# Two chained convolution layers on one core: the last three channel groups taken image by image, early loads in parts, outputs in blocks of 1024 columns

## The chip, the core and the metric

The kernel runs on one core of a Trainium2 chip. The metric is the device time of one execution in microseconds. Its engines are TensorE (PE in the profile; PEld is its weight load), VectorE (DVE), ScalarE (ACT), GpSimd (POOL) and SyncE (SP); 16 DMA engines move data between HBM and the on-chip memory (SBUF). SyncE, GpSimd and ScalarE can issue DMAs, each in the order of its own instructions.

## The reference

Input x is 4 images of 64 channels, 256 x 256, float32. Layer 0 is a long convolution: two small sine networks give, for every channel, a filter along the rows and one along the columns, and their outer product is convolved with the image through an FFT of double size; a bias times x is added. Layer 1 whitens the 64 channels: a covariance of every ninth pixel, its inverse square root by five Newton-Schulz steps, and a 64 x 64 product with every pixel.

```python
k = jnp.einsum('ijk,imk->ijmk', hx, hy)[0]
y = jnp.fft.irfft2(u_f * k_f, s=(fft_size, fft_size))[..., :L, :L]
out = y + x * bias[:, None, None]
...
x1 = jnp.transpose(x, (1, 0, 2, 3)).reshape(B, -1)
x1_s = x1[:, ::STRIDE ** 2]
mean1 = jnp.mean(x1_s, axis=-1, keepdims=True)
xc = x1 - mean1
cov = x1_s @ x1_s.T / x1_s.shape[1] + EPS * jnp.eye(B, dtype=x.dtype)
deconv = _isqrt_newton_schulz(cov, N_ITER)
out = deconv @ xc
```

## The kernel before, in words

**Layer 0.** The separable convolution is done as two products with Toeplitz matrices for each channel of each image. The work is cut in 32 steps (lines 107 and 108), a step being one group of 8 channels (index g, 0 to 7) of one image (n, 0 to 3). Groups 0 to 5 go group by group, all four images inside; groups 6 and 7 go image by image. Each step has four items of two channels (c = 0, 2, 4, 6). `group` (line 394) makes TensorE do the first product of one item together with the second product of the item two places before, so that an item is finished two groups after it was begun. A place is written (step, c), as in the table `early`. ScalarE copies the first products (line 409), VectorE adds x times the bias to the second ones, in place of x (line 412).

**Around it.** After each group SyncE's queue gets, in this order: two stores of the finished item to a DRAM scratch `y_d` (line 425, 1 KB a row), a load of two channels of x for the step two ahead, into one of four tiles (line 588), perhaps an eighth of a later group's Toeplitz matrices (line 594, by the table `blocks`, line 371) and perhaps an early load of the second layer (line 596, by the table `early`, line 378). The matrices lie in three tiles. VectorE also picks the pixels for the covariance by masked copies (line 319), which `pack` (line 385) hands out by a budget of 2.92 for each group. The covariance of an image (line 333, on TensorE) is placed one step behind the image's last group (line 571).

**Between the layers.** After the last item, TensorE picks the last pixels by products (line 300), makes the last covariance and goes through the Newton-Schulz chain (`whitening`, line 460), which gives W and a shift.

**Layer 1.** The 32 pieces (line 344) are 128 x 4096 numbers of `y_d` each, 2 MB: the two image halves by 64 channels as rows. For blocks of columns, four products with W fill two banks (line 635), ScalarE and VectorE add the shift and write them back in place (lines 639, 640), and the piece is stored to the output (line 645). The on-chip tiles of layer 0 that are done with serve as the homes of the pieces (line 347): 13 at a time, from the pools of the matrices (t), the samples (s), x (i) and one more (e). Nine of the first 13 are loaded by `early` before layer 0 ends, the others on line 614. Piece 13 and on is loaded (line 647) when the piece 13 before it has been stored. The outputs of piece 0 and of the last 13 are issued by SyncE, the others by GpSimd. A piece is 2 x 2048 columns: block w takes 512 of each half. Outputs go out in 4 DMAs for piece 0, 2 for piece 1 and for the last two, 1 for the others.

Of the kernel before, what the change touches and what calls it, by code (L numbers as in the profile page):

```python
# [38 lines left out]
F32 = mybir.dt.float32  # L39
I32 = mybir.dt.int32  # L40
AF = mybir.ActivationFunctionType
ALU = mybir.AluOpType
# [3 lines left out]
NB, C, L = 4, 64, 256  # L46
P, H2 = 128, 2
EMB, ORDER = 33, 64
PIX = L * L
CG = 8  # L50
# [4 lines left out]
EPS = 0.01  # L55
N_ITER = 5
GW = P + L
FP = 4096

TURN = 6.283185  # L60
# [4 lines left out]
def conv_whiten_kernel(ctx: ExitStack, tc: tile.TileContext, a: dict, out: bass.AP):  # L65
    nc = tc.nc
    x = a["x"]

    const = ctx.enter_context(tc.tile_pool(name="const", bufs=1))
    xpool = ctx.enter_context(tc.tile_pool(name="xpool", bufs=4))  # L70
    epool = ctx.enter_context(tc.tile_pool(name="epool", bufs=2))
    spool = ctx.enter_context(tc.tile_pool(name="spool", bufs=NB))
    tpool = ctx.enter_context(tc.tile_pool(name="tpool", bufs=3))
    o1pool = ctx.enter_context(tc.tile_pool(name="o1pool", bufs=4))
# [13 lines left out]
    cols = const.tile([P, 4], F32, tag="cols", name="cols")  # L88
# [9 lines left out]
    bias = const.tile([P, C], F32, tag="bias", name="bias")  # L98

    def load_x(t, g, n, c):  # L100
        nc.sync.dma_start(
            out=t[:, c : c + 2],
            in_=x[n, g][:, c : c + 2],
        )


    steps = [(g, n) for g in range(C // CG - 2) for n in range(NB)]
    steps += [(g, n) for n in range(NB) for g in range(C // CG - 2, C // CG)]

    x_tiles = [xpool.tile([P, CG, H2, L], F32, tag="in", name=f"x{u}") for u in range(4)]  # L110
    for c in range(0, CG, 2):
        load_x(x_tiles[0], *steps[0], c)
# [8 lines left out]
    for n in range(NB):  # L121
        t = spool.tile([P, FP], F32, tag="samp", name=f"samp{n}")
        samp.append(
# [31 lines left out]
    for i in range(3):  # L155
        for u in range(2):
# [3 lines left out]
            arg, k, nxt = (scratch[:, 2 + 3 * i + v, half] for v in range(3))  # L160
# [166 lines left out]
    def covariance(n):  # L327
# [15 lines left out]

    pieces = [(n, q) for n in range(NB) for q in range(PIX // H2 // FP)]


    homes = [
        {"t": (tpool, "toep"), "s": (spool, "samp"), "i": (xpool, "in"), "e": (epool, "extra")}[k]
        for k in "eetssiistitis"
    ]  # L350

    def load_y(i):
# [4 lines left out]
        nc.sync.dma_start(out=t, in_=y_d[n][:, q * FP : (q + 1) * FP])  # L357
        return t

    def load_next():  # L360
        loaded[len(loaded)] = load_y(len(loaded))

    loaded = {}
    todo = []
# [16 lines left out]
    orders = [list(range(L // HP)), list(reversed(range(L // HP)))]  # L381

# [174 lines left out]
    with tc.manual_schedule(  # L557
        engines={engines.PE, engines.SP, engines.DVE, engines.Activation, engines.Pool}
    ):
        toep = {0: new_toeplitz(0)}  # L560

        for f, lo, hi in ((0, 0, 2), (0, 2, 4), (0, 4, 6), (1, 0, 2), (0, 6, 8), (1, 2, 4), (1, 4, 8)):
            for half in range(2):
                load_toeplitz(toep[0], 0, f, half, lo, hi, nc.scalar if half else nc.sync)
        for c in range(0, CG, 2):
            load_x(x_tiles[1], *steps[1], c)
        for i, (g, n) in enumerate(steps):
            xt = x_tiles[i % 4]
            for c in range(0, CG, 2):
                item = (g, n, c, xt, [])  # L570
                if g == C // CG - 1 and n > 0 and c == 2:
                    covariance(n - 1)
                if len(pending) == 2:
                    group(item, pending.pop(0))
                else:
                    half_group(item, 0)
                pending.append(item)
                if i == 0 and c == 6:

                    fold = const.tile([P, C], F32, tag="fold", name="fold")  # L580
# [8 lines left out]
                if (i, c) in blocks:  # L589
                    tg, part = blocks[i, c]  # L590
# [24 lines left out]
        W, shift = whitening(i15, ones)  # L615


    halves = [slice(u * C, (u + 1) * C) for u in range(2)]
    for i, (n, q) in enumerate(pieces):
        yt = loaded.pop(i)  # L620

        v = yt.rearrange("p (v f) -> p v f", v=2)
        o = out[n, q].rearrange("p (v f) -> p v f", v=2)

        part = 512 if i == 0 else 1024 if i == 1 or i > len(pieces) - 3 else 2048
        for w in range(FP // 1024):


            cols = slice(w * 512, (w + 1) * 512)
            po = [  # L630
                psA.tile([P, 512], F32, tag="psA", name=f"po_{n}_{q}_{w}_{u}") for u in range(2)
            ]
            for k in range(2):
                for u in range(2):
                    nc.tensor.matmul(  # L635
                        po[u][halves[k]], lhsT=W[halves[u]], rhs=v[halves[u], k, cols],
                        start=True, stop=True,
                    )
            nc.scalar.activation(v[:, 0, cols], po[0], AF.Identity, bias=shift)  # L639
            nc.vector.tensor_scalar(v[:, 1, cols], po[1], shift, None, ALU.add)  # L640
            end = (w + 1) * 512
            if end % part == 0:

                issue = nc.sync if i == 0 or i + len(homes) >= len(pieces) else nc.gpsimd
                issue.dma_start(out=o[:, :, end - part : end], in_=v[:, :, end - part : end])  # L645
        if i + len(homes) < len(pieces):
            loaded[i + len(homes)] = load_y(i + len(homes))

# [57 lines left out]
```

## Time and profile before

| what | value |
|---|---|
| median of 3 runs | 902.66 us (902.32 to 902.82) |
| span of the profiled execution | 902.1 us |
| TensorE matmul busy | 781.2 us (87%) |
| VectorE busy | 581.5 us (64%) |
| ScalarE busy | 395.5 us (44%) |
| bytes moved by DMA | 285.61 MB, mean 317 GB/s |
| x loads (line 101) | 128 of 512 KB, median 5.3 us from issue to landing |
| `y_d` stores (line 425) | 256 of 256 KB, median 3.5 us |
| piece loads (line 357) | 32 of 2 MB, median 15.6 us |

The profile is one execution. It gives for each engine the busy time, in 40 equal slices of the span too; a chain of what released what, followed back from the end; groups of instructions by line with the idle time before them; and DMA traffic by queue and by issue. A busy share of one engine over the whole span says little here, since the two layers load the engines differently; the slices show that. "Share" of the DMA engines is the mean busy share of the 16. The profile's own execution is not among the three timed runs; its span counts from the first to the last instruction.

### The profile page before, as it was taken

The numbers are of one execution on the slowest core, as the hardware profiler recorded it, in microseconds if no ns is written. First come the engines' busy times: TensorE is split into PE (matmuls) and PEld (weight loads), VectorE is DVE, ScalarE is ACT, GpSimd is POOL, SyncE is SP. The second block draws the span as 40 slices with busy tenths as digits, with TensorE's granted clock in tenths as the row PEclk, the third lists the DMA queues.
The fourth block names the chain that finished last, engine by engine and source line by source line (L and its number), as shares of the span: only waits on it lengthen the run. The fifth ranks groups of instructions, "written<-read, shape, count | busy, mean of one in ns | idle before, by whom it ended". The sixth has DMA issues, their size and how long they took to land.

```text
span 902.1 us, 28046 instructions
## 1 busy us (share of the span) xinstructions
PE 781.2 (87%) x11928; PEld 647.5 (72%) x11928; DVE 581.5 (64%) x801; ACT 395.5 (44%) x676; POOL 14.5 (2%) x40
## 2 busy tenths in 40 slices
PE   8999999999999999999999999999999565666200
PEld 7999999999999999999999999999533111212000
DVE  3487778877888778877888877877688332233200
ACT  2655554545455555545454444442487232233200
POOL 1000000000000000000000000000010000000000
PEclk9999999999999999999999999999999766866755
DMA  7988889798788888888997899979999999999998
GB/s 209 327 262 252 242 261 271 234 273 251 247 263 261 244 264 259 258 250 267 293 275 241 285 351 356 335 237 390 375 401 429 430 432 432 429 434 430 430 430 355
DMA packets 117912, 285.61 MB, mean 317 GB/s; under 512 B 8891, under 2 KB 91116, under 8 KB 110108
## 3 DMA queue, kind: packets, MB, share of 16 engines
q1 hardware_dynamic: 113436, 244.94, 79.0%
q0 software_dynamic: 3056, 37.95, 10.0%
q8 instruction: 95, 1.56, 0.7%
q10 hardware_dynamic: 1296, 0.93, 0.4%
q14 instruction: 29, 0.24, 0.1%
HBM read 149.35 MB, written 134.44 MB: 315 GB/s over the span
## 4 chain that ended last, share of the span: by engine, by line
PE 74%; DMA 11%; another core or an unknown queue 7%; DVE 0%; issue 0%; SPq 0%; ACT 0%; POOLq 0%; DVEq 0%
PE p L220 64%; DMA out_dram<-yi 5%; DMA yi<-y_d 5%; PE po L635 4%; PE pc L333 2%; PE ph L252 1%; PE pk L300 1%; PE spin L442 1%; DMA toep<-g_d 0%; PE busy L152 0%; PE pm L158 0%; SPq L357 0%; DMA scratch<-in_zw_dram 0%; DVE yi L640 0%
## 5 line engine op out<-in xcount | busy, mean ns | idle before, releaser
L220 PE MATMUL p<-toep,x 64*64 64x64 f32 (+3 forms) x5040 | 579.5, 284 | 0.8 <-issue 0.8
L220 PE MATMUL p<-toep,o 64*64 64x64 f32 (+3 forms) x5040 | 579.5, 284 | 0.0
L220 PEld LDWEIGHTS p<-toep,x 64*128 64x128 f32 (+1 forms) x5040 | 535.7, 166 | 24.4 <-issue 1.3
L220 PEld LDWEIGHTS p<-toep,o 64*128 64x128 f32 (+1 forms) x5040 | 536.7, 166 | 10.7 <-issue 0.2
L409 ACT COPY o<-p 64x512 f32<-64x512 f32 x504 | 292.8, 581 | 294.2 <-PE p L220 286.6
L319 DVE COPY_PREDICATED samp<-mask,x 128x464 f32<-128x464 int32 (+3 forms) x351 | 297.2, 847 | 9.8 <-DVE x L412 0.2
L412 DVE SCALAR_TENSOR_TENSOR x<-x,bias,p 128x512 f32<-128x512 f32 x252 | 179.8, 744 | 121.3 <-PE p L220 117.3
L635 PE MATMUL po<-yi,chain 64*64 64x512 f32 x1024 | 143.7, 720 | 60.4 <-DMA yi<-y_d 60.4
L640 DVE TENSOR_SCALAR yi<-po,shift 128x512 f32<-128x512 f32 x128 | 96.1, 751 | 109.0 <-PE po L635 100.7
L635 PEld LDWEIGHTS po<-yi,chain 64*64 64x64 f32 x1024 | 48.0, 162 | 155.2 <-issue 150.5
L639 ACT ACTIVATE yi<-po,shift 128x512 f32<-128x512 f32 x128 | 88.0, 687 | 116.7 <-PE po L635 116.0
L333 PE MATMUL pc<-samp 128*64 128x65 f32 x464 | 14.9, 223 | 0.0
L333 PEld LDWEIGHTS pc<-samp 128*64 128x64 f32 x464 | 14.3, 137 | 0.3
L645 POOL DMA_DIRECT2D out_dram<-yi x19 | 10.5, 554 | 130.5 <-DMA out_dram<-yi 55.1
L606 POOL TENSOR_SCALAR chain<-ident 64x64 f32<-64x64 f32 x2 | 1.0, 519 | 606.6 <-PE ph L252 606.6
L286 DVE COPY o<-ph 64x256 f32<-64x256 f32 x8 | 3.4, 422 | 9.7 <-PE ph L252 9.6
L152 PE MATMUL busy<-idle 128*128 128x128 f32 x64 | 9.4, 307 | 0.0
L152 PEld LDWEIGHTS busy<-idle 128*128 128x128 f32 x64 | 8.9, 222 | 0.2 <-issue 0.2
L300 PE MATMUL pk<-x,pick 128*128 128x56 f32 (+1 forms) x72 | 8.3, 292 | 0.0
L300 PEld LDWEIGHTS pk<-x,pick 128*128 128x128 f32 x72 | 8.1, 192 | 0.1
L442 PE MATMUL spin<-ident 128*128 128x128 f32 x50 | 7.9, 292 | 0.0
L286 ACT COPY o<-ph 64x256 f32<-64x256 f32 x8 | 2.9, 368 | 10.7 <-DMA toep<-g_d 9.2
(93 smaller groups left out, 77.4 us busy)
## 6 DMA issues: line engine op xcount, KB each, us to landing
x<-in_x_dram SPq DMA_DIRECT2D x128, 512.0 KB, 5.3
y_d<-x SPq DMA_DIRECT2D x256, 256.0 KB, 3.5
yi<-y_d SPq DMA_DIRECT2D x32, 2048.0 KB, 15.6
out_dram<-yi POOLq DMA_DIRECT2D x17, 2048.0 KB, 67.7
out_dram<-yi SPq DMA_DIRECT2D x11, 2048.0 KB, 32.9
toep<-g_d SPq DMA_DIRECT2D x28, 256.0 KB, 6.3
toep<-g_d SPq DMA_DIRECT2D x29, 192.0 KB, 5.7
out_dram<-yi SPq DMA_DIRECT2D x4, 1024.0 KB, 32.8
```

Of the source, the lines that this page charges most:

```text
L152: nc.tensor.matmul(p, lhsT=idle[:, 0:P], rhs=idle[:, P : 2 * P], start=True, stop=True)
L220: mm = nc.tensor.matmul(ps[q : q + w, m, HP * k : L], lhsT=src[parts, k // 2, m * P + q : m * P + q + w], rhs=t[parts, : stop : -1] if k e ...
L300: nc.tensor.matmul(pk[:, b, :, 0:nj], lhsT=pick[:, (s - b) % STEP, :], rhs=yt[:, cs, b, s : s + STEP * (nj - 1) + 1 : STEP], start=(s == 0 ...
L319: nc.vector.copy_predicated(dst, m, src)
L333: nc.tensor.matmul(pc[half], lhsT=samp[n][:, b, j, 0:C], rhs=samp[n][:, b, j, :], start=(b == 0 and j < 2), stop=(b == H2 - 1 and j >= NJ ...
L409: nc.scalar.copy(o1[to], units[u][0][0][fr])
L412: nc.vector.scalar_tensor_tensor(x2[:, c2 + u], x2[:, c2 + u], bias[:, ch : ch + 1], units[u][1][0], ALU.mult, ALU.add,)
L442: nc.tensor.matmul(p, lhsT=ident, rhs=ident, start=True, stop=True)
L635: nc.tensor.matmul(po[u][halves[k]], lhsT=W[halves[u]], rhs=v[halves[u], k, cols], start=True, stop=True,)
L639: nc.scalar.activation(v[:, 0, cols], po[0], AF.Identity, bias=shift)
L640: nc.vector.tensor_scalar(v[:, 1, cols], po[1], shift, None, ALU.add)
L645: issue.dma_start(out=o[:, :, end - part : end], in_=v[:, :, end - part : end])
```

## The change

- Groups 5, 6 and 7 go image by image, not 6 and 7 alone: image 0 is complete after 23 steps instead of 26. The covariance of an image stays one step behind its last group.
- x has three tiles instead of four, and is loaded one step ahead instead of two; x of the last step is loaded in the first half of step 30. The pool `e` has three tiles instead of two.
- The tables change: Toeplitz blocks of groups 4 to 7 are loaded earlier (and two at a time in places for group 7), in another order of their eight parts; ten pieces are loaded early, the first at (23,4), instead of nine from (26,4). Those before step 30 are loaded in four DMAs of 1024 columns each.
- A piece is cut in four blocks of 1024 adjacent columns, a block being 2 x 512. A slice of the output is then contiguous in each row. The number of output DMAs of each piece stays.

```diff
+LATE = 3
-    xpool = ctx.enter_context(tc.tile_pool(name="xpool", bufs=4))
-    epool = ctx.enter_context(tc.tile_pool(name="epool", bufs=2))
+    xpool = ctx.enter_context(tc.tile_pool(name="xpool", bufs=3))
+    epool = ctx.enter_context(tc.tile_pool(name="epool", bufs=3))
...
-    steps = [(g, n) for g in range(C // CG - 2) for n in range(NB)]
-    steps += [(g, n) for n in range(NB) for g in range(C // CG - 2, C // CG)]
+    steps = [(g, n) for g in range(C // CG - LATE) for n in range(NB)]
+    steps += [(g, n) for n in range(NB) for g in range(C // CG - LATE, C // CG)]
...
+    def x_of(i):
+        return x_tiles[(i + 1) % 3]
...
-        for k in "eetssiistitis"
+        for k in "eeessstititis"
...
-        nc.sync.dma_start(out=t, in_=y_d[n][:, q * FP : (q + 1) * FP])
+        width = FP // parts
+        for at in range(0, FP, width):
+            nc.sync.dma_start(
+                out=t[:, at : at + width], in_=y_d[n][:, q * FP + at : q * FP + at + width]
+            )
...
-    for g in range(1, C // CG):
-        first = 16 * g - 14 if g < C // CG - 1 else 16 * g - 22
-        for part in range(8):
-            k = first + (part * 12 // 8 if g < C // CG - 2 else part)
-            blocks[k // 4, k % 4 * 2] = (g, part)
+    for g, (first, groups) in {
+        1: (2, 12), 2: (18, 12), 3: (34, 12), 4: (46, 12), 5: (57, 12), 6: (69, 12), 7: (82, 5)
+    }.items():
+        for at, part in enumerate((0, 2, 1, 3, 4, 6, 5, 7)):
+            k = first + at * groups // 8
+            blocks.setdefault((k // 4, k % 4 * 2), []).append((g, part))
...
-        (26, 4): 1, (27, 0): 1, (27, 4): 1, (28, 0): 1, (29, 2): 1, (30, 0): 1, (31, 0): 1, (31, 2): 1, (31, 4): 1
+        (23, 4): 1, (24, 0): 1, (24, 4): 1, (25, 0): 1, (27, 2): 1, (30, 2): 1, (30, 4): 1, (31, 2): 2, (31, 6): 1
...
-                if g == C // CG - 1 and n > 0 and c == 2:
+                if g == C // CG - 2 and n > 0 and c == 2:
                     covariance(n - 1)
...
-                if i + 2 < len(steps):
-                    load_x(x_tiles[(i + 2) % 4], *steps[i + 2], c)
+                if 0 < i < len(steps) - 2:
+                    load_x(x_of(i + 1), *steps[i + 1], c)
+                elif i == len(steps) - 2 and c < CG // 2:
+                    for ahead in (2 * c, 2 * c + 2):
+                        load_x(x_of(i + 1), *steps[i + 1], ahead)
...
-                    load_next()
+                    load_next(4 if i < len(steps) - 2 else 1)
...
-        v = yt.rearrange("p (v f) -> p v f", v=2)
-        o = out[n, q].rearrange("p (v f) -> p v f", v=2)
-        part = 512 if i == 0 else 1024 if i == 1 or i > len(pieces) - 3 else 2048
+        v = yt.rearrange("p (w v f) -> p w v f", v=2, f=512)
+        part = 1024 if i == 0 else 2048 if i == 1 or i > len(pieces) - 3 else 4096
...
-                        po[u][halves[k]], lhsT=W[halves[u]], rhs=v[halves[u], k, cols],
+                        po[u][halves[k]], lhsT=W[halves[u]], rhs=v[halves[u], w, k],
...
-                issue.dma_start(out=o[:, :, end - part : end], in_=v[:, :, end - part : end])
+                issue.dma_start(out=out[n, q][:, end - part : end], in_=yt[:, end - part : end])
```

More of the change, by code (lines that the diff above doesn't have):

```diff
@@ L104, in load_x @@
         )
-    steps = [(g, n) for g in range(C // CG - 2) for n in range(NB)]
-    steps += [(g, n) for n in range(NB) for g in range(C // CG - 2, C // CG)]
-    x_tiles = [xpool.tile([P, CG, H2, L], F32, tag="in", name=f"x{u}") for u in range(4)]
+    steps = [(g, n) for g in range(C // CG - LATE) for n in range(NB)]
+    steps += [(g, n) for n in range(NB) for g in range(C // CG - LATE, C // CG)]
+    x_tiles = [xpool.tile([P, CG, H2, L], F32, tag="in", name=f"x{u}") for u in range(3)]
+    def x_of(i):
+        return x_tiles[(i + 1) % 3]
     for c in range(0, CG, 2):
-        load_x(x_tiles[0], *steps[0], c)
+        load_x(x_of(0), *steps[0], c)
         if c == 0:
@@ L348, in conv_whiten_kernel, with load_y @@
         {"t": (tpool, "toep"), "s": (spool, "samp"), "i": (xpool, "in"), "e": (epool, "extra")}[k]
-        for k in "eetssiistitis"
+        for k in "eeessstititis"
     ]
-    def load_y(i):
+    def load_y(i, parts=1):
         n, q = pieces[i]
@@ L356, in load_y, with load_next @@
         t = pool.tile([P, FP], F32, tag=tag, name=f"yi_{n}_{q}")
-        nc.sync.dma_start(out=t, in_=y_d[n][:, q * FP : (q + 1) * FP])
-        return t
-    def load_next():
-        loaded[len(loaded)] = load_y(len(loaded))
+        width = FP // parts
[3 more added lines that the diff above has]
+            )
+        return t
+    def load_next(parts=1):
+        loaded[len(loaded)] = load_y(len(loaded), parts)
     loaded = {}
@@ L565, in conv_whiten_kernel @@
         for c in range(0, CG, 2):
-            load_x(x_tiles[1], *steps[1], c)
+            load_x(x_of(1), *steps[1], c)
         for i, (g, n) in enumerate(steps):
-            xt = x_tiles[i % 4]
+            xt = x_of(i)
             for c in range(0, CG, 2):
                 item = (g, n, c, xt, [])
-                if g == C // CG - 1 and n > 0 and c == 2:
+                if g == C // CG - 2 and n > 0 and c == 2:
                     covariance(n - 1)
@@ L585, in conv_whiten_kernel @@
                     load_pick(c // 2 * 3, c // 2 * 3 + 3)
-                if i + 2 < len(steps):
-                    load_x(x_tiles[(i + 2) % 4], *steps[i + 2], c)
-                if (i, c) in blocks:
-                    tg, part = blocks[i, c]
+                if 0 < i < len(steps) - 2:
[3 more added lines that the diff above has]
+                        load_x(x_of(i + 1), *steps[i + 1], ahead)
+                for tg, part in blocks.get((i, c), ()):
                     if part == 0:
@@ L620, in conv_whiten_kernel @@
         yt = loaded.pop(i)
-        v = yt.rearrange("p (v f) -> p v f", v=2)
-        o = out[n, q].rearrange("p (v f) -> p v f", v=2)
-        part = 512 if i == 0 else 1024 if i == 1 or i > len(pieces) - 3 else 2048
+        v = yt.rearrange("p (w v f) -> p w v f", v=2, f=512)
+        part = 1024 if i == 0 else 2048 if i == 1 or i > len(pieces) - 3 else 4096
         for w in range(FP // 1024):
-            cols = slice(w * 512, (w + 1) * 512)
             po = [
@@ L635, in conv_whiten_kernel @@
                     nc.tensor.matmul(
-                        po[u][halves[k]], lhsT=W[halves[u]], rhs=v[halves[u], k, cols],
+                        po[u][halves[k]], lhsT=W[halves[u]], rhs=v[halves[u], w, k],
                         start=True, stop=True,
                     )
-            nc.scalar.activation(v[:, 0, cols], po[0], AF.Identity, bias=shift)
-            nc.vector.tensor_scalar(v[:, 1, cols], po[1], shift, None, ALU.add)
-            end = (w + 1) * 512
+            nc.scalar.activation(v[:, w, 0], po[0], AF.Identity, bias=shift)
+            nc.vector.tensor_scalar(v[:, w, 1], po[1], shift, None, ALU.add)
+            end = (w + 1) * 1024
             if end % part == 0:
                 issue = nc.sync if i == 0 or i + len(homes) >= len(pieces) else nc.gpsimd
-                issue.dma_start(out=o[:, :, end - part : end], in_=v[:, :, end - part : end])
+                issue.dma_start(out=out[n, q][:, end - part : end], in_=yt[:, end - part : end])
         if i + len(homes) < len(pieces):
@@ L702 @@
     r = run_bass_kernel_spmd(nc, [arrays], core_ids=[0])
-    y = np.asarray(r.results[0]["out_0_dram"]).reshape(NB, PIX // H2 // FP, H2, C, H2, FP // 2)
-    return np.ascontiguousarray(y.transpose(0, 3, 4, 1, 2, 5)).reshape(NB, C, L, L)
+    y = np.asarray(r.results[0]["out_0_dram"]).reshape(NB, PIX // H2 // FP, H2, C, FP // 1024, H2, 512)
+    return np.ascontiguousarray(y.transpose(0, 3, 5, 1, 4, 2, 6)).reshape(NB, C, L, L)
```

## The prediction

> **What bounds the kernel now.** I read the 40 slices of the page first, then the chain that ended last, then the busy times by stretch, SyncE's timeline and the DMA traffic by queue.
>
> ```profile
> PE   8999999999999999999999999999999565666200
> DMA  7988889798788888888997899979999999999998
> ```
>
> The first is TensorE, the second the 16 DMA engines. TensorE is full until about slice 31 (700 us) and not after; DMA is full at the end. So there are two stages with two limits. The chain in order of time shows where the first gives way:
>
> ```profile
> 83.73 430.31 PE p L220 x7458
> ...
> 520.70 0.47 issue
> ...
> 643.25 27.70 PE po L635 x256
> ```
>
> Columns: start, duration, what. From 22.51 to 632.2 us the chain is TensorE with hardly a gap, so the convolution (line 220) sets when the whitening matrix W is ready (643.25 us). What follows is DMA:
>
> ```profile
> core 0: us, PE busy (x) PEld busy (x) DVE busy (x) ACT busy (x) POOL busy (x), PEclk, DMA share, GB/s
> 599.00:645.00 46.00, 44.83 (x615) 40.37 (x613) 28.12 (x70) 10.24 (x27) 1.15 (x3) 1.00 0.99 382
> 645.00:647.00 2.00, 2.00 (x24) 0.72 (x20) 1.75 (x4) 1.54 (x4) 0.00 (x0) 1.00 0.20 77
> 647.00:652.00 5.00, 5.00 (x52) 1.84 (x48) 4.45 (x6) 4.02 (x6) 1.04 (x2) 1.00 1.02 382
> 656.00:664.00 8.00, 8.00 (x80) 2.91 (x76) 7.04 (x10) 6.36 (x10) 1.08 (x2) 1.00 1.02 354
> 664.00:890.00 226.00, 122.84 (x835) 40.50 (x824) 78.86 (x106) 72.18 (x105) 7.48 (x14) 0.73 1.01 430
> 890.00:898.00 8.00, 0.00 (x0) 0.00 (x0) 0.00 (x0) 0.00 (x0) 0.00 (x0) 0.50 1.01 416
> ```
>
> After W, 32 pieces must be written and the 19 that have no home yet must be loaded: 51 x 2.097 MB = 107.0 MB. The stretches from 647 to 902 hold 107.1 MB (rate by length, 652 to 656 at 386 GB/s and 898 to 902 at 73 included). So nothing but these 51 pieces is left at 647 us, and the end is 647 plus their transfer time. The 13 early loads are through before that: DMA falls to 0.20 between 645 and 647, and the first output is issued in that hole:
>
> ```profile
> 622.10 10.46 SPq L357 DMA_DIRECT2D yi<-y_d  x4
> 645.57 3.51 SPq L645 DMA_DIRECT2D out_dram<-yi  x4
> ```
>
> **The change part by part.** The span is 902.1 us; the median of the runs is 902.66, 0.56 more, which I take to stay.
>
> *Image by image, ten early pieces instead of nine.* The homes stay 13, so after W there are still 51 pieces. Loading the tenth before the convolution ends takes one 4.9 us transfer out of 622 to 645 us, where it delays nobody: the DMA engines are then idle some 5 us longer before the first output, which waits for W. Cost and gain zero. What hides it is TensorE's work up to 643 us. TensorE, VectorE and ScalarE get the same number of instructions in another order; the covariance of an image stays one step behind its last group, and the last twelve mask copies and their places among the last groups are the same, so W is not later for their sake. The Toeplitz loads come earlier, twice two within one step of four groups for the last channel group; between 400 and 470 us of before, one per group ran at a mean DMA share of 0.93, so two exceed a group's 4.6 us by under a microsecond each, which the lead of x covers.
>
> *Packets of the outputs.* The new column order makes a slice of an output contiguous: 4 KB instead of 2 KB a row for piece 0, 8 instead of 4 for piece 1 and the last two; the other 28 stay at 16 KB. Prices, from the traffic by queue (packets, MB, share of 16 engines) in 645 to 653, 653 to 660, 890 to 898 and 700 to 720 us:
>
> ```profile
> q1 hardware_dynamic: 1101, 2.18, 73.4%
> ```
>
> ```profile
> q0 software_dynamic: 476, 1.88, 78.8%
> ```
>
> ```profile
> q1 hardware_dynamic: 866, 3.33, 101.4%
> ```
>
> ```profile
> q1 hardware_dynamic: 295, 4.31, 50.3%
> q0 software_dynamic: 297, 4.26, 49.8%
> ```
>
> 2 KB: 0.734 x 16 x 8 us / 1101 = 85 ns a packet. 4 KB on GpSimd's queue: 0.788 x 16 x 7 / 476 = 185 ns. 4 KB on SyncE's: 1.014 x 16 x 8 / 813 = 160 ns (without 53 packets under 512 B). 16 KB: 1.001 x 16 x 20 / 523 = 612 ns (without 69). A piece then takes, on each of 16 engines: 64 x 85 = 5.46 us, 32 x 185 = 5.94, 32 x 160 = 5.11, 8 x 612 = 4.90. The trace has no 8 KB output. It lies between 4.90 and the 4 KB price; on the straight line through 160 and 612 it is 311 ns, 16 x 311 = 4.97.
> - Piece 0: 5.46 to 5.11, -0.35.
> - Piece 1: 5.94 to something from 4.90 to 5.94. On SyncE's price it would gain 0.97; but 26 ns of the 185 may belong to its place beside the first 16 KB load, and stay (16 x 337 = 5.39, gain 0.55). I take the middle, -0.76.
> - The last two: 2 x (5.11 - 4.97) = -0.28; at most 0.42.
>
> All of this is on the path: the share is 1.01 or more throughout. Sum -1.39, bounds 0 (8 KB no better, 4 KB beside other traffic no better) to -1.81.
>
> *Four parts.* The early pieces before step 30 go as 4 KB packets: 5.11 us instead of 4.90 each, beside TensorE's work, and four issues of about 0.4 us instead of one on SyncE, which waits most of the time for VectorE. No cost as long as x comes in time. The gain may be in TensorE's small holes. Groups end alternately 3.93 and 5.22 us apart (ScalarE's first copies); between 507 and 585 us, with early loads running, three gaps are 0.78, 0.32 and 0.15 us too long; from 84 to 514 us, with x and Toeplitz blocks alone, the chain has no hole. The chain calls the largest "issue", that is, no wait. Bounds: gain 1.25, or a loss of 0.5 if more and smaller requests hold TensorE up as well (three such holes at most, by the 0.15 row). I take -0.5, as only five of ten pieces are split.
>
> The Trainium skill's page "Runtime: NRT & Kernel Launch", section "Instruction fetch mechanics", says that instructions are streamed in 16 KiB blocks through a DMA queue, at a cost mostly hidden. By it this term would be about 0. The trace has such a queue (95 packets, 1.56 MB); that it made these holes is not shown.
>
> The page "DMA: Bandwidth & Descriptors" wants transfers of 1 MiB or more (section "Bandwidth"), and its fit has 2 us fixed per transfer (section "Anatomy of one DMA"): by it, as an estimate, four parts of 512 KB take 12.8 us instead of 6.8, and x would be late. Here the four 512 KB outputs of piece 0 ran at a share of 1.02, back to back, so the fixed part overlaps.
>
> *x one step ahead instead of two, three tiles.* The tile that is overwritten is that of three steps earlier than the one loaded, last stored six groups before, so the load has nothing new to wait for. Queued behind it on SyncE are the next group's y stores. But its lead halves. The tightest load of before:
>
> ```profile
> 534.86 0.42 SPq L101 DMA_DIRECT2D x<-in_x_dram  x1
> ```
>
> ```profile
> DMA to landing us min/median/max: 10.0/10.0/10.0
> ```
>
> ```profile
> 531.92 2.40 ACT L409 COPY o<-p 64x512 f32<-64x512 f32 x4 [1.88 <-PE p L220]
> 537.14 2.37 ACT L409 COPY o<-p 64x512 f32<-64x512 f32 x4 [2.82 <-PE p L220]
> 541.07 2.40 ACT L409 COPY o<-p 64x512 f32<-64x512 f32 x4 [1.56 <-PE p L220]
> 546.29 2.37 ACT L409 COPY o<-p 64x512 f32<-64x512 f32 x4 [2.82 <-PE p L220]
> ```
>
> With a lead of four groups it would be wanted when the fourth of these groups has ended, at 546.3; it landed at 544.9. That leaves 1.4 us. The new loads fall on (23,4), (24,0), (24,4), (25,0) with a covariance at (24,2): the pattern of before, (26,4) to (28,0) with one at (27,2), moved by three whole steps. So this row is also the tightest of after, less 0.2 us for the 4 KB packets. Cost 0; without the cover, what exceeds 1.2 us. x of the last step goes two chunks at a time in step 30, ahead of the single loads.
>
> Sum: -1.39 - 0.5 = -1.9: 902.1 to 900.2 of span, 902.66 to 900.8 of median. About 0.2% (1.8 us) is what a measurement of this kernel can tell from no change, so the forecast stands at that edge.
>
> **Rivals.**
> - *The packets give less, and the holes stay* (within 0.2%): piece 1 gains 0.55 or nothing, TensorE's gaps are not of the 16 KB loads: -0.6 to -1.2, some 901.7. For it: the hole's cause is only guessed.
> - *x is late* (slower): the 4 KB parts or the doubled Toeplitz blocks lengthen the landing beyond 11.4 us from issue. TensorE then stalls for the excess at every chunk behind a split piece, five pieces, one or two chunks each; an excess of 0.5 to 1 us over five to eight chunks is 2.5 to 8, less the 1.4 of the outputs, about +1 to +6.5, middle 906. It decides from a mean landing 1.4 us longer than the tightest of before. Against it: most landings in that stretch were 4.3 to 8.7 us.
> - *The tenth early piece counts in full*: if the early loads were still running when outputs start, one less would give 4.88 us more, 896. Against it: the hole at 645 to 647.
>
> **How the numbers follow.** Forecast 0.40, less gain 0.35, x late 0.17, the extra piece 0.08. Faster by over 0.2%: 0.48; within: 0.35; slower: 0.17. Range: down to -3.1 (1.81 and 1.25), 899.5; up to a mild case of late x, 904.2. That leaves out the extra piece and the worse half of late x.
>
> **What would show it.** Right: DMA idle for about 7 us before 647 us, first output still issued at 645 to 646; the first stretch of outputs near 400 GB/s instead of 382 and 354; fewer "issue" gaps on line 220. Wrong: TensorE waiting for x on line 220 between 460 and 560 us, W later than 643, or a tail shorter than 250 us.

## The result, and the profile after

The kernel after takes **904.88 us** (median of 13 runs, 903.85 to 907.39), the kernel before 902.66 (median of 13, 901.38 to 903.57). The ratio is 1.0030, with a 95% interval of 1.0022 to 1.0038: slower by 0.3%, where 0.2% faster was forecast, and 0.7 us above the range. The profiled execution has a span of 903.1 us and took 905.11.

The 40 slices of the page look as before (TensorE, then the DMA engines):

```profile
PE   8999999999999999999999999999999566556300
DMA  7798788788888898889799878699899999999998
```

The loss does not show at this grain. The chain that ended last, in order of time (start, duration, what), shows one part of it:

```profile
22.00 435.23 PE p L225 x7585
457.23 3.64 PE pc L338 x116
460.87 0.49 PE p L225 x18
461.36 1.63 issue
462.99 55.45 PE p L225 x931
...
642.70 27.70 PE po L645 x256
```

Line 225 holds the products (220 before), 338 the covariance, 645 the products with W. Right behind the first covariance TensorE does 18 matmuls and then nothing for 1.63 us, in the middle of a run of like matmuls, and the chain finds no semaphore that it waits for. TensorE never waits for x. W is ready at 642.70 us, 0.55 earlier than in before, as the products began 0.5 us earlier in this execution. From the first product of layer 0 to the first with W both profiled executions take 620.9 us, so these two alone don't show what the stall costs; the experiments do.

The busy times by stretch show the other part (columns as in the prediction; the last two are DMA share and GB/s):

```profile
646.00:650.00 4.00, 4.00 (x44) 1.40 (x40) 3.46 (x6) 3.15 (x6) 0.00 (x0) 1.00 1.01 405
650.00:656.00 6.00, 6.00 (x63) 2.13 (x58) 5.25 (x8) 4.80 (x8) 1.67 (x3) 1.00 0.61 203
656.00:664.00 8.00, 8.00 (x80) 2.90 (x76) 7.04 (x10) 6.46 (x10) 1.06 (x2) 1.00 1.00 388
664.00:890.00 226.00, 122.21 (x828) 40.75 (x820) 78.43 (x105) 71.68 (x105) 7.46 (x14) 0.75 1.01 430
890.00:898.00 8.00, 0.00 (x0) 0.00 (x0) 0.00 (x0) 0.00 (x0) 0.00 (x0) 0.50 1.01 429
```

Between 650 and 656 us the DMA engines are 0.61 busy and move 203 GB/s. The kernel before had 1.01 and 384 in these six microseconds:

```profile
650.00:656.00 6.00, 6.00 (x60) 2.14 (x56) 5.25 (x8) 4.80 (x8) 1.97 (x3) 1.00 1.01 384
```

39% of 6 us are 2.3 us of the resource that bounds this stage. What was not there to be moved are the outputs of piece 1, as GpSimd's timeline shows (start, duration, what, in brackets the idle time before it and what it is put down to):

```profile
652.72 1.14 POOL L655 DMA_DIRECT2D out_dram<-yi  x2 [33.11 <-ACT yi L649]
```

Both outputs go out in one run of 1.14 us, the first 10.0 us after the first product with W. In before they went out 1.66 us apart, as the results came, the first 6.8 us after that product:

```profile
650.03 0.73 POOL L645 DMA_DIRECT2D out_dram<-yi  x1 [29.80 <-ACT yi L639]
651.69 0.69 POOL L645 DMA_DIRECT2D out_dram<-yi  x1 [0.92 <-DVE yi L640]
```

The profile puts the wait down to ScalarE, but its results were there: GpSimd's waiting instruction ended at 648.90 us, and its next instruction starts at 652.70. In this gap of 3.8 us lie three packets of 8 KB on the instruction queue q14, at 649.7 and 651.0 (two); in before, q14 has no packet between 646.3 and 652.5.

So there are two losses, and neither is a wait for data. The theories of the first four experiments: **A**, GpSimd's late output costs the time; **B**, the new blocks of columns cost it; **C**, the new order and the early loads cost it.

### The profile page after: what moved, and what is told of

Same layout as the page of the kernel before. It is cut to its first block, busy times and chain, and to the rows that moved or that the text cites. A ratio compares the mean times of both kernels' runs of the same rounds, so it can differ in the third digit from the quotient of the medians.

```text
span 903.1 us, 28052 instructions
## 1 busy us (share of the span) xinstructions
PE 780.3 (86%) x11928; PEld 647.1 (72%) x11928; DVE 580.6 (64%) x801; ACT 395.1 (44%) x676; POOL 14.1 (2%) x40
## 4 chain that ended last, share of the span: by engine, by line
PE 73%; another core or an unknown queue 11%; DMA 8%; DVE 1%; issue 1%; SPq 0%; ACT 0%; POOLq 0%; DVEq 0%
PE p L225 64%; DMA out_dram<-yi 5%; PE po L645 4%; DMA yi<-y_d 2%; PE pc L338 2%; PE ph L257 1%; PE pk L305 1%; PE spin L452 1%; SPq L364 0%; DMA toep<-g_d 0%; PE busy L157 0%; PE pm L163 0%; DMA scratch<-in_zw_dram 0%; DVE yi L650 0%
## 5 line engine op out<-in xcount | busy, mean ns | idle before, releaser
L225 PEld LDWEIGHTS p<-toep,o 64*128 64x128 f32 (+1 forms) x5040 | 536.1, 166 | 10.5
L655 POOL DMA_DIRECT2D out_dram<-yi x19 | 10.2, 536 | 130.7 <-DMA out_dram<-yi 48.9
```

Source lines behind the costliest of these rows:

```text
L225: mm = nc.tensor.matmul(ps[q : q + w, m, HP * k : L], lhsT=src[parts, k // 2, m * P + q : m * P + q + w], rhs=t[parts, : stop : -1] if k e ...
L655: issue.dma_start(out=out[n, q][:, end - part : end], in_=yt[:, end - part : end])
```

## The experiments

Fifteen kernels, each timed in five rounds beside the kernel before on the same chip (the medians of before there are 902.41 to 902.72). The columns of the table: time from the first product of layer 0 to the first with W; the time TensorE stood still, without waiting, in the first covariance or up to 4 us behind it; from the first product with W to GpSimd's first output; the place of that output among GpSimd's instructions, counted in the program; from the first product with W to the end of the span. These five are of the profiled execution, the last two of all runs.

| kernel | to W, us | stall, us | GpSimd's first output after | its place | W to end, us | median, us | ratio [95%] |
|---|---|---|---|---|---|---|---|
| before | 620.9 | 0.47 | 6.8 | 836 | 258.9 | 902.66 | 1 |
| after | 620.9 | 1.63 | 10.0 | 837 | 260.4 | 904.88 | 1.0030 [1.0022, 1.0038] |
| e1_blocks_only | 619.6 | 0.2 | 6.8 | 836 | 258.4 | 902.03 | 0.9994 [0.9986, 1.0003] |
| e2_piece1_sync | 621.2 | 1.48 | 11.9 (piece 2) | 838 | 258.5 | 903.93 | 1.0013 [1.0004, 1.0022] |
| e3_whole_loads | 622.6 | 2.22 | 6.8 | 836 | 258.3 | 904.81 | 1.0026 [1.0016, 1.0036] |
| e4_order_only | 621.3 | 1.84 | 10.3 | 837 | 261.8 | 907.00 | 1.0044 [1.0031, 1.0056] |
| f1_pool_shift | 621.1 | 1.26 | 6.8 | 861 | 257.8 | 903.73 | 1.0012 [1.0002, 1.0021] |
| f2_split_cov | 619.7 | 0 | 10.2 | 837 | 260.7 | 903.98 | 1.0016 [1.0007, 1.0024] |
| f3_loads_later | 619.1 | 0 | 10.0 | 837 | 260.5 | 902.44 | 0.9999 [0.9991, 1.0008] |
| f4_pe_shift | 620.5 | 1.78 | 10.5 | 837 | 259.7 | 908.10 | 1.0058 [1.0046, 1.0070] |
| g1_both | 620.3 | 0.41 | 6.8 | 861 | 257.8 | 900.95 | 0.9984 [0.9976, 0.9993] |
| g2_sync_later | 619.5 | 0 | 11.9 (piece 2) | 838 | 259.0 | 901.81 | 0.9991 [0.9983, 1.0000] |
| g3_before_pad1 | 620.4 | 0.52 | 10.4 | 837 | 261.4 | 905.74 | 1.0035 [1.0022, 1.0047] |
| g4_both_old_blocks | 619.5 | 0 | 6.8 | 861 | 258.9 | 901.58 | 0.9988 [0.9979, 0.9997] |
| h1_both_whole | 619.0 | 0 | 6.8 | 860 | 258.0 | 901.26 | 0.9984 [0.9975, 0.9992] |
| h2_old_order_parts | 620.8 | 0.9 | 6.8 | 861 | 258.0 | 901.43 | 0.9986 [0.9977, 0.9995] |
| i1_pe_back | 620.2 | 0.78 | 10.0 | 837 | 259.9 | 904.30 | 1.0023 [1.0014, 1.0032] |

### First four: which part of the change costs

**e1_blocks_only**: before, with the blocks and outputs of 1024 columns alone (the last part of the diff).

> The kernel before with only the second layer's blocks of 1024 columns (4 KB and 8 KB output rows); order, tiles and early loads as before. Theory A (the changed kernel lost its gain because GpSimd issues the first output of piece 1 some 3.2 us late, 652.7 instead of 649.5, and the DMA engines stand at a share of 0.61 for 6 us): this kernel has one load for each early piece, so GpSimd has no added waits; piece 1 is issued in time, no hole, and the packets bring what was priced: 1.0 to 1.8 us less than before. Theory B (the new column blocks themselves cost): 0.5 us or more above before, with the hole. Theory C (the order and the loads cost, the blocks do nothing): equal to before within 0.4 us.

Measured 902.03. B falls: GpSimd is on time and the blocks cost nothing. They bring 0.4 us, which is within theory C's 0.4 and less than the 1.0 to 1.8 of theory A; the interval includes no change.

**e4_order_only**: the rest of the change, with before's blocks.

```
-        v = yt.rearrange("p (w v f) -> p w v f", v=2, f=512)
+        v = yt.rearrange("p (v f) -> p v f", v=2)
```

> The other half: the order of the last three groups, three tiles of x, the early loads in four parts, with the second layer in its old form of 512 columns of each half. Theory A: the extra waits of GpSimd come with the loads in parts, so the hole is here, about 2.3 us, and the 2 KB and 4 KB outputs too: 2 to 3.5 us above before. Theory B: equal to before within 0.5 us. Theory C: 2 us or more above before, but with holes in TensorE's convolution (over 1.5 us in sum on the line of the products) and not at 650 us.

Measured 907.00, 4.6 us above before and more than the 2 to 3.5 of theory A. GpSimd is late and TensorE stalls without the new blocks, so both come with the order and the loads.

**e2_piece1_sync**: after, with piece 1's outputs on SyncE.

```
-                issue = nc.sync if i == 0 or i + len(homes) >= len(pieces) else nc.gpsimd
+                issue = nc.sync if i < 2 or i + len(homes) >= len(pieces) else nc.gpsimd
```

> The changed kernel with the two outputs of piece 1 issued by SyncE, whose queue stands ready after piece 0, in place of GpSimd. Theory A: DMA stays full from 646 to 656 us, and the time falls by 1.8 to 2.8 us against the changed kernel (904.9 to about 902.5); GpSimd's first issue, now of piece 2, may be late without cost, as piece 1 covers it. Theories B and C: no change within 0.5 us.

Measured 903.93. The DMA share of 650 to 656 us is 1.03 and W to end 1.9 us shorter in the profiled execution: A holds. The median fell by 0.9 us only, where 1.8 to 2.8 were expected, and the kernel stays slower than before, so A is not all.

**e3_whole_loads**: after, with each early piece in one DMA.

```
-                    load_next(4 if i < len(steps) - 2 else 1)
+                    load_next()
```

> The changed kernel with every early piece loaded by one DMA. Theory A in its first form (the loads in four parts give GpSimd more waits, and these make it late): the hole goes, 1.8 to 2.8 us less than the changed kernel. If GpSimd is late for another reason (where its instructions are cut into blocks for fetching), the hole may stay, and the time with it. For TensorE: if 16 KB packets make its holes in the convolution, they grow from 1.6 us to over 2; if not, they stay below 2.

Measured 904.81, where theory A gave 1.8 to 2.8 us less than after. GpSimd is on time, so its lateness comes of the four parts. But TensorE's stall is longer, 2.22 us, and the granted clock (third column from the right) falls after it:

```profile
464.00:466.00 2.00, 2.00 (x28) 1.88 (x29) 0.00 (x0) 0.00 (x0) 0.00 (x0) 0.50 1.15 456
466.00:468.00 2.00, 2.00 (x22) 2.00 (x22) 0.00 (x0) 0.00 (x0) 0.00 (x0) 0.69 1.03 437
```

At 0.50 and 0.69 over 4 us some 1.6 us of clock are lost besides the stall (an estimate); the time to W is 1.7 us longer than in after, 0.6 of it the longer stall. With stalls up to 1.84 us the clock stayed at 1.00 in these stretches (after, e2, e4, f1, f4).

### Second four: what makes GpSimd late, and TensorE stand still

**f1_pool_shift**: after, with nothing changed but GpSimd's instructions ahead of the wait.

```
         nc.gpsimd.memset(ones, 1.0)
+        idle = const.tile([1, 1], F32, tag="idle", name="idle")
+        for _ in range(24):
+            nc.gpsimd.memset(idle, 0.0)
```

> The kernel after, with 24 memsets of one element put on GpSimd right after the memset of ones at 620 us, where GpSimd then waits some 30 us for the first results; nothing else is changed, and nothing of the loads. Theory A2 (GpSimd has reached the end of a block of instructions just between the wait that ended at 648.9 us and its first output at 652.7; two requests on the instruction queue q14, at 649.7 and 651.0, lie in that gap): the blocks' ends move to other instructions, piece 1's first output is issued 6.8 us after the first layer-2 product instead of 10.0, the DMA share between 650 and 656 us of after's time goes from 0.61 to about 1.0, and the time falls by 1.0 to 1.5 us, to 903.4 to 903.9. Rival (the four loads' semaphores themselves, or the queue's state, make GpSimd late): the output still comes 10 us after the first product, and the time stays at 904.9.

Measured 903.73. GpSimd's timeline:

```profile
650.17 0.61 POOL L658 DMA_DIRECT2D out_dram<-yi  x1 [26.47 <-DVE yi L653]
```

W came at 643.41 here, so the first output is 6.8 us behind it. Instructions that do nothing took the lateness away, with loads, semaphores and queues as they were.

**f2_split_cov**: after, with the covariances of images 0 to 2 in two halves, a group of products between them.

```
-                    covariance(n - 1)
+                    covariance(n - 1, (0,))
...
+                if g == C // CG - 2 and n > 0 and c == 2:
+                    covariance(n - 1, (1,))
                 pending.append(item)
```

> The kernel after, with the covariance of an image in two halves of 58 matmuls, one ahead of a group of products and one behind it, instead of 116 in a row (three times; a second addition of 0.23 us on VectorE each time). Theory S (TensorE's 116 short matmuls with 116 weight loads in 3.64 us use up instructions faster than the instruction queue brings them; TensorE then stands still for 1.6 us at 461 without waiting for a semaphore): the stall at 461 goes or falls under 0.5 us, W comes 1.1 to 1.6 us earlier, time 903.3 to 903.8. Rival L (the early pieces' loads delay what TensorE needs, whatever the covariance): a stall of 1 to 2 us stays between 455 and 475 us, time 904.5 to 905.

Measured 903.98, 0.2 above the range, with W 1.2 us earlier and no issue gap on the product line in the whole of layer 0:

```profile
457.47 1.89 PE pc L338 x58
459.36 4.79 PE p L225 x80
464.15 1.89 PE pc L338 x58
```

**f3_loads_later**: after, with four early pieces moved away from the first covariance.

```
-        (23, 4): 1, (24, 0): 1, (24, 4): 1, (25, 0): 1, (27, 2): 1, ...
+        (25, 0): 1, (25, 4): 1, (26, 0): 1, (26, 4): 1, (27, 2): 1, ...
```

> The kernel after, with the first four early pieces issued at steps (25,0), (25,4), (26,0), (26,4) instead of (23,4), (24,0), (24,4), (25,0), so that none of them runs between 440 and 470 us, where the first covariance is. Rival L: the stall of 1.6 us at 461 goes, time about 903.3. Theory S with the DMA load as a part of it (the block of instructions has to pass the queues behind the early pieces): stall falls to 0 to 0.8. Theory S without it: stall of 1 to 2 us stays, time 904.5 to 905. A new wait for x between 475 and 515 us is possible in this kernel, as early loads run there up to the next covariance; the chain will tell it apart.

Measured 902.44. The covariance as a whole, and no stall behind it; a smaller one comes at 489.66 us, in the middle of products, where early pieces now run:

```profile
457.05 3.64 PE pc L338 x116
460.70 28.97 PE p L225 x520
489.66 0.51 issue
```

The DMA share of 456 to 460 us is 0.68 here and 0.99 in after. TensorE's own instruction queue (q8, packets of 16 KB) fits: ahead of the stall its packets start at 450.4 and 460.7 us in after, at 449.9 and 457.6 in f3. The second one is 3 us later where early pieces fill the DMA engines, and after's TensorE goes on 2.3 us behind it.

**f4_pe_shift**: after, with 88 instructions more on TensorE ahead of layer 0.

```
-    busy(22)
+    busy(44, P // 2)
```

> The kernel after, with the 22 idle matmuls of 128 columns ahead of the first Toeplitz products replaced by 44 of 64 columns: 88 more instructions on TensorE at about the same busy time, so that every later end of a block of instructions falls on an instruction some 88 earlier; nothing else is changed. Theory S with alignment as its main part (it matters where in a block the covariance begins): the stall at 461 changes by more than 0.8 us, to either side, and another covariance may show one. Without alignment: 1.4 to 2.0 us stay at 461. Rival L: unchanged too. Time 903.3 if the stall goes, 904.9 if it stays.

Measured 908.10, of which some 4 us are a fault of the experiment: a matmul of 64 columns took as long as one of 128 (9.77 us for 88, 4.91 for 44), and the products began 4.0 us late. The stall is there, but elsewhere:

```profile
461.24 2.89 PE pc L340 x91
464.12 1.78 issue
465.90 0.97 PE pc L340 x25
```

In after it came 18 matmuls behind the covariance, here 25 ahead of its end: 43 matmuls, with their weight loads 86 instructions, against 88 added. The stall sits at a fixed place in TensorE's stream of instructions. Its size hardly changed, though, and the forecast that alignment would change it by 0.8 us fell; the last experiment takes that up.

### Third four: both repairs, and the test the other way round

**g1_both**: after with the edits of f1 and f3.

> The kernel after with both repairs: 24 memsets of one element behind that of ones on GpSimd, and the first four early pieces at (25,0), (25,4), (26,0), (26,4). If the two losses are separate: W at 640.9 us as with the loads later alone (no stall at 461), first output of piece 1 6.8 us after the first layer-2 product, and from there 258 us to the end as with the memsets alone: span 899.0, time 900.7 to 901.4, faster than before by 0.1 to 0.2%. If one loss takes the place of the other (W earlier, but the transfers before it not done, so that the outputs wait): 902.4 as with the loads later alone.

Measured **900.95**, 0.9984 [0.9976, 0.9993]: faster than both kernels. The losses add up. Ratios: 1.0030 for after, less 0.0018 by f1's edit and 0.0031 by f3's, makes 0.9981 against 0.9984 measured.

**g2_sync_later**: f3's edit with e2's.

> The kernel after with the first four early pieces later, and piece 1's two outputs issued by SyncE instead of the memsets on GpSimd. The same W at 640.9 and no hole between 648 and 655 us, since SyncE has no such end of a block there and piece 2 is issued later than GpSimd is late: 900.7 to 901.8. If the place of a queue matters beside the lateness (piece 1 behind piece 0 on one queue), up to 0.5 us more than with the memsets.

Measured 901.81; not told apart from g1_both, as the intervals overlap.

**g3_before_pad1**: the kernel before with one memset of one element more.

```
         nc.gpsimd.memset(ones, 1.0)
+        idle = const.tile([1, 1], F32, tag="idle", name="idle")
+        for _ in range(1):
+            nc.gpsimd.memset(idle, 0.0)
```

> The kernel before with one memset of one element more on GpSimd, at the same place, so that piece 1's first output is GpSimd's instruction 837 as in after, and not 836. Theory A2 (only the place of the instruction in GpSimd's stream decides): the output is issued 9.5 to 10.5 us after the first layer-2 product instead of 6.8, a hole in the DMA work of 650 to 656 us appears (share 0.6 to 0.7), and the kernel before becomes slower by 1.0 to 1.5 us, 903.5 to 904.0. Rival (the loads in four parts are needed, by their semaphores or their queue): on time, no hole, 902.5.

Measured 905.74, **3.2 us more**: slower as theory A2 said, but by about twice its 1.0 to 1.5. GpSimd's timeline and the stretch:

```profile
653.09 2.04 POOL L648 DMA_DIRECT2D out_dram<-yi  x3 [33.37 <-ACT yi L642]
```

```profile
650.00:656.00 6.00, 6.00 (x60) 2.14 (x56) 5.25 (x8) 4.80 (x8) 2.00 (x3) 1.00 0.71 247
```

Three outputs in one run, 10.4 us behind W: the hole of after, in the kernel before, with its own loads. The rival falls: the four parts are not needed for the lateness. In after they bring it by one more waiting instruction ahead of the output.

**g4_both_old_blocks**: g1_both with before's blocks.

> After's order and loads with both repairs, but before's blocks of 512 columns of either half and its outputs in 2 KB and 4 KB rows at the start. Beside the kernel with both repairs it prices the new blocks where nothing else stands in their way: by the prediction's packets 1.39 us more (902.1 to 902.8); by what the blocks alone gave on the kernel before, 0.4 to 0.6 more (901.2 to 901.9).

Measured 901.58, 0.6 above g1_both: the blocks are worth little in the time.

### Two more: where g1_both's gain over before comes from

**h1_both_whole**: g1_both with e3's edit (whole early pieces).

> The kernel with both repairs, but each early piece in one DMA of 2 MB instead of four of 512 KB, as in the kernel before; GpSimd's memsets stay, so that it is not late either way. This prices the four parts by themselves. By the prediction's term (TensorE's holes come from the 16 KB packets): 0.5 us more than with both repairs, 901.4, with TensorE issue gaps of 0.5 to 1.3 us on the product line. If the holes are of the DMA load as such: no difference beyond 0.3 us, 900.7 to 901.3, gaps as with both repairs (0.9 us in all).

Measured 901.26, the same ratio as g1_both, and no issue gap in layer 0, where both forecasts had some. The four parts by themselves bring nothing that can be measured.

**h2_old_order_parts**: before's order and early loads, with new blocks, four parts and the memsets.

> The order and the early loads of before (last two channel groups image by image, nine early pieces, x two steps ahead in four tiles), with the new blocks, the early pieces in four parts and the 24 memsets on GpSimd. Beside the kernel with both repairs it prices the new order. If the order costs and brings nothing, as predicted: 900.9 to 901.5. If the new order brings what is left (0.6 to 1.1 us between before and the kernels with both repairs that the blocks do not explain): 901.8 to 902.2, as with the blocks alone on before.

Measured 901.43, 0.9986. The order by itself brings or costs nothing that can be measured. Of g1_both's 1.4 us below before, 0.4 to 0.6 are then the blocks; the rest is not assigned to any part.

### The last: why before stalls less with the same loads

Before has the same early loads around the same covariance, three steps later and at a DMA share of about 1.0 too, and yet stalls of 0.2 to 0.9 us (e1, before, g3, h2) against 1.26 to 2.22 (after, e2, e3, e4, f1, f4). The trace gives the starts of the 256 matmuls and weight loads that end at the stall, about one packet of 16 KB: they take 4.89 us in before's order, where they end 63 matmuls behind the covariance, and 3.76 to 3.79 us in the six others. So f4 had moved the stall from one equally dense stretch to another.

**i1_pe_back**: after, with 64 instructions fewer on TensorE.

```
-    busy(22)
+    busy(6, 0, 4 * P)
```

> The kernel after, with the 22 idle matmuls of 128 columns ahead of the first Toeplitz products replaced by 6 of 512 columns: 64 instructions fewer on TensorE before layer 0, nothing else changed. In the profiles so far, the 256 instructions that end at the stall lasted 4.89 us in the order of before (they end 63 matmuls behind the covariance) and 3.76 to 3.79 us in the new order and in the kernel with 88 instructions more (they end 18 behind it, and 25 ahead of its end); the stalls were 0.2 to 0.9 against 1.26 to 2.22. If it is the time that the block in work gives the next one to arrive, the stall comes 50 matmuls behind the covariance here, the 256 instructions last about 4.6 us, the stall falls by about 0.85 us, to 0.4 to 1.4, and the time by as much or more, to 903.4 to 904.2. If the order of the groups as such makes the stall longer (another kind of rival: more traffic in that stretch), it stays at 1.3 to 2.2, wherever it lies, and the time at 904.9.

```profile
457.47 3.64 PE pc L340 x116
461.12 2.04 PE p L227 x50
463.15 0.78 issue
```

The stall is 50 matmuls behind the covariance and falls by 0.85 us to 0.78, as forecast; the 256 instructions take 4.27 us, where 4.6 were forecast. By this one profile the order as such does not make it longer. The median, 904.30, is 0.1 above the range; it fell by 0.6 against after's, but the intervals overlap. GpSimd is late here too.

Two more things in the traces tie the stalls to TensorE's instruction queue. TensorE stood still without a wait for over 0.15 us 21 times between 50 and 626 us, in 15 of the 17 kernels. Counted from the first record of TensorE's stream, its sequencer's included, all 21 come at the same place, 193 behind a multiple of 256; in after, 24288 records and 94 packets make 258 a packet. And TensorE goes on 2.2 to 2.5 us after the start of a packet on q8 in 19 of them (2.6 and 3.1 us in the other two). In f2 the packet started as late as in after, at 461.05 us, but the block ahead of it, with products between the two halves of the covariance, lasted until 463.68, and nothing was lost. Seven of the 21, of 0.3 to 0.8 us, lie among products alone; so the burst is needed for the long stalls and not for every stall.

## Why the prediction was wrong

**Image by image, ten early pieces: "cost and gain zero". Here it failed first.** The step asked whom the early loads delay and looked only at data: W, x, the Toeplitz blocks. It did not ask for TensorE's own instructions, which come through the same DMA engines. A covariance takes 116 matmuls and 116 weight loads in 3.64 us; in the stretch before, 100 to 440 us, the packets of 16 KB started some 7 us apart (7.2 by the median in after). With early pieces filling the DMA engines the next packet started at 460.69 us instead of 457.63 (f3), too late for this block. Shown: the stalls of over a microsecond need the dense matmuls (f2) and the early pieces at that moment (f3), and they move with the instructions (f4, i1). By f3 against after it costs 0.0031 of the time, 2.8 us, with an uncertainty of about 1 (1.8 us of the time to W in the profiled executions); the profiled stalls are 1.3 to 2.2, and e3 shows that a longer one costs its clock as well. Four of the 13 runs of after have spans of 904.7 to 905.6 us, the other nine 902.1 to 903.2; whether those four lost the clock was not seen.

The prediction's sentence "the pattern of before ... moved by three whole steps" is where it went astray: the loads moved with the covariance, the ends of TensorE's blocks of instructions did not. In before the block that ends behind the covariance gives the next one 4.89 us to arrive, in after 3.76 (i1 in between). From when a block is asked for, no trace shows; from the start of its packet to TensorE's next instruction it was 2.2 to 2.5 us.

**Four parts: "-0.5", from TensorE's small holes.** Both holes of before's products, 0.37 and 0.47 us, are stalls of that kind, at the same place in a block of 256. Whether the early loads go in packets of 4 or of 16 KB made no difference in the time (h1_both_whole against g1_both). In single profiles the stall was longer with whole loads beside the covariance (e3 against after) and absent with whole loads moved away (h1 against g1), so an effect on its size is not shown. The step counted SyncE's four issues, but not what the loads leave behind: each DMA has a completion that the later output waits for, one more waiting instruction on GpSimd in front of it, and that put the output at place 837. The table's seven kernels at 837 are all late by 3.2 to 3.7 us; those at 836, 860 and 861 are on time. By f1 against after this costs 0.0018, 1.6 us (2.6 from W to the end in the profiled executions); by g3, 3.2 us where outputs are in 512-column blocks. That GpSimd was waiting for its instructions is inferred from the q14 packets in the gap; that the place decides is shown, for these four places. No rival of the prediction had it.

The Trainium skill's page "Runtime: NRT & Kernel Launch", section "Instruction fetch mechanics", calls the cost of crossing a block of instructions mostly hidden, and the prediction let that stand against the 95 packets in its profile. For most blocks these runs agree: no kernel shows more than three stalls of over 0.15 us in layer 0, with 94 or 95 packets each. They differ for the few: 0.2 to 2.2 us on TensorE's critical path, and 3.2 to 3.7 us at GpSimd's first output.

**Packets: "-1.39".** The prices held. Summed over the packets by size and queue: piece 0 from 5.65 to 5.25 us on each engine (-0.40, forecast -0.35); piece 1 from 6.07 to between 5.16 and 5.80 in the six kernels with GpSimd on time (-0.3 to -0.9, forecast -0.76); the last two from 416 to 429 GB/s, 10.08 to 9.78 us for 4.19 MB (-0.30, forecast -0.28). W to end, with GpSimd on time: 258.9 twice with the old blocks, 257.8 to 258.4 in six kernels with the new ones, so 0.5 to 1.1 us less. The medians show 0.4 (e1 on before) and 0.6 (g4 to g1), each with some 0.8 of uncertainty. The term was right in sign and mechanism, and somewhat large, as the DMA engines were not full throughout the first outputs: 0.87 between 644 and 648 us in g1.

**x one step ahead: 0.** Right: TensorE never waited for x on the product line in any of the profiles, even with early pieces moved (f3). My slow rival, x late, was the right sign by the wrong mechanism.

**What would show it.** "DMA idle for about 7 us before 647" failed: the engines were at 1.00 from 632 to 644. First output at 645 to 646: 644.70. First outputs near 400 GB/s: 405 between 646 and 650, and then the hole. Fewer issue gaps on the product line: one instead of two, but 1.63 us instead of 0.84.

**The 0.56 us around the span** did not stay. Time less span was 1.7 to 2.4 us in every run that gave both, mostly 1.8. So before's profiled execution, with 902.1 of span, was some 1.2 us slower than its median one, and 0.8 us of its holes need not have been in the median, from which I took 0.5 off.

## What to carry to other kernels

Instructions are a transfer too: where a burst of short matmuls meets large loads that are in no hurry, move the loads or break up the burst (2.8 and 1.3 us here), and suspect it where the chain says "issue" in the middle of like matmuls. Splitting a DMA adds completions that a later instruction on another engine waits for; read that engine's order, not only the issuing one's. Before a small loss is put down to the edit, shift the late engine's instructions by a few that do nothing: if the loss goes, it was the place and not the edit.

## What the runs showed of the hardware

- One memset of one element on an idle engine made the kernel before 3.2 us slower (g3), by the place of one later instruction.
- TensorE's stalls lie at one place in blocks of 256 instructions (all 21), and it goes on 2.2 to 2.5 us after a packet of its instruction queue has started (19 of 21).
- A stall of 2.22 us on TensorE was followed by a granted clock of 0.50 and 0.69 over the next 4 us (e3, one profile); behind stalls of 1.26 to 1.84 us it stayed at 1.00. The page "TensorE: Matmul & The Clock Gate", section "Part 1: The HAM clock gate", has the clock fall after an idle window of about 3.4 us; here, in this one profile, 2.22 us were enough.
- Among the idle matmuls ahead of layer 0, each with its weight load, 64-column ones took 111 ns each, as 128-column ones did (f4).
